# A relational graph layer on one core: S1 T1 by quarters in more calls, and B21 with its sum T4 taken later

## Chip, core and metric

The kernel runs on one core of one Trainium2 chip. The metric is the device time of one execution in microseconds (us); lower is better. The core has a matrix engine (TensorE, PE in the profile; its weight loads are PEld), VectorE (DVE), ScalarE (ACT), GpSimd (POOL) and SyncE (SP). SP, ACT and POOL also issue DMA transfers.

## What is computed

1250 nodes with 1024 features each, 20,000 edges of 8 types. The reference, cut to what matters:

```python
h = jnp.maximum(_layernorm(x, axis=-1), 0.0)
out = h @ root + bias
for r in range(8):
    mask = (edge_type == r).astype(h.dtype)
    sums = jax.ops.segment_sum(h[src] * mask[:, None], dst, num_segments=1250)
    cnt = jax.ops.segment_sum(mask, dst, num_segments=1250)
    out = out + (sums / jnp.maximum(cnt, 1.0)[:, None]) @ weight[r]
u = out
z = jnp.concatenate([u, h], axis=1) @ w_gate + b_gate
result = x + jnp.tanh(u) * z + h * (1.0 - z)
```

Everything is float32. The kernel multiplies first and gathers afterwards: it computes `h @ weight[r]` for all nodes, stores the products in HBM (`y`), and then gathers, for each node, one product row per edge and adds it with its weight.

## The kernel before, in words

**Matrices.** Eleven matrices of 1024 x 1024 are taken one after the other, s = 0 to 10: the eight relation weights (s = 0 to 7), `root` (s = 8), and the two halves of `w_gate` (s = 9, 10). In words they are called matrix one to matrix eleven, so matrix six is s = 5. `R0 = (0, 5, 8)` splits the relations into two groups for the gather: five and three. `EARLY` is 3, `NM` 11, `NP` 5.

**Calls.** The node rows are ten blocks of 128. One call `step(s, i)` with i = 0 to 4 multiplies the block pair (i, i + 5) by matrix s; the first call is i = 0. Each call runs `product`, which is Strassen's scheme in Winograd's form: with the pair's rows as [A11 A12; A21 A22] and the matrix as [B11 B12; B21 B22], all quarters 512 wide, seven products are made in place of eight. The left sums (S1 to S4) were made once and stay in `h_op`; the right sums are made by VectorE for each matrix: T1 = B12 − B11, T2 = B22 − T1, T3 = B22 − B12, T4 = B21 − T2 (`make_t1` to `make_t4`, one instruction each, lines 195 to 207). The products are A11 B11, A12 B21, S1 T1, S2 T2, S3 T3, S4 B22 and A22 T4.

**Where the quarters lie.** Nine buffers of 1 MB hold them. B21 goes into the buffer in which the matrix before had T3; T4 goes into the one in which the matrix before had B22. `load_first`, `load_next`, `load_b22` and `load_b21` bring B11, B12, B22 and B21 of the next matrix during the fourth and fifth call of the present one; the loads of B11, B22 and B21 leave on ScalarE's DMA queue, that of B12 on SP's. In the code, `load_b21` is called at (i, j) = (4, 3) and `make_t4` at (0, 1) of the matrix itself.

**By quarters.** From matrix two on, two calls that follow each other (i = 0 and 1, i = 2 and 3) are paired, and for the two block pairs together some of the seven products are split once more in the same scheme, with 256-wide quarters and seven small products for what would be eight: A12 B21 (class `Second`), S4 B22 (class `Third`, `thirds(s)`, from matrix five on), A11 B11 (class `First`) and S1 T1 (class `Fifth`). `fifths(s, i)` says for which calls the last holds. `Fifth` has a head part, which runs in the first call of the two (`begin`, `second`, `early`, `late`, with `sums` and `next_sums` on VectorE), and leaves the bank `to1` for the other call. In `product` its object is `root`, `Third`'s is `inner`, and `head` is true for i = 0 and 2.

**Banks.** `narrow` is set to `fifths(s, i)`. With it, one of the four rotating PSUM banks is kept (`sum_bank`, `kept`, and `touch`, a short matmul that opens it); without it the bank is given back.

**Order of the work.** All engines run in the order in which the program is written. The schedule is by hand: `product` calls `done()` after each of its products, and `done()` calls `between(j)` with j = 0, 1, 2 and so on. Here that is `beside(j)` in `step`, which places loads, right sums, and the sums of the smaller schemes, and then calls the outer `between`, which places what belongs to the edges. Two more hooks matter. `filled(name)` runs the matmuls of a smaller scheme beside a named product, and makes a further break where that returns true. `between(TICK)` with `TICK` = 9 is an extra break in the head part of a call with `root`.

**First call, from matrix six on.** In order on TensorE: `root.begin()`, the end of `First` (`first.late()`, the bank of p1), `root.second()`, break 0, S2 T2, break 1, `root.early()`, `e.second()` (a quarter product of A12 B21), break 2, S3 T3, the extra break, `root.late()`, break 3, `q.second()` (a quarter product of S4 B22), break 4, A22 T4, break 5. At break 2 and 5 VectorE makes the right sums of `Second` out of B21 (`sums(j)`, line 231); at break 3 it makes the sums of `Third` (`q.sums()`, lines 309 to 312).

**Edges.** While matrices six to eight are multiplied, the rows of the first group are gathered; while nine and ten are multiplied, those of the second. GpSimd issues one indirect DMA for each slot (line 1562, 512 KB, into one of five buffers `got`), and VectorE adds it with a weight to `u` (line 1567). `spread` hands these steps out over the breaks: each break of a call adds 10, 8, 13, 11 or 8 units (by i), and the steps advance to their share of all units; for the first group 123 steps are spread over 1050 units, for the second 88 over 700. On SP run the stores of the products (`put`, line 731), the loads of the bias or of kept partial sums into `u` (line 1580) and the loads of kept left sums (line 243).

Of the kernel before, what the change touches and what calls it, by code (L numbers as in the profile page):

```python
# [21 lines left out]
def tile_rgcn_highway(  # L22
# [44 lines left out]
    NP = ND // 2  # L67
# [3 lines left out]
    R0 = (0, 5, R)  # L71
    K = ((28, 14, 13, 12, 11, 10, 9, 8, 7, 6), (20, 10, 8, 7, 7, 6, 5, 5, 4, 3))
    EARLY = 3
# [10 lines left out]
    TICK = 9  # L84
    LEFTS_AT = 6
    FIFTHS = (1, 4)
# [59 lines left out]
    def lead():  # L146

        return psum.tile([P, 512], F32, name="ps_b", bufs=2)
# [346 lines left out]
    def product(aop, w, to, between=lambda j: None, last=None, pieces=1, whole=True,  # L495
# [13 lines left out]
        def add(b, i, fresh=False, at=slice(0, Q), ks=range(KQ)):  # L509
            for k in ks:  # L510
                nc.tensor.matmul(b[:, at], aop[:, i, k, :], w.of[i][:, k, at],  # L511
                                 start=(fresh and k == 0), stop=(k == KQ - 1),
                                 skip_group_check=True)

        def done():
            between(step[0])
            step[0] += 1

        def filled(name):
            if fill and name in fill and fill[name]():  # L520
                done()
                return True
            return False
# [39 lines left out]
        def p1():  # L563
            if first is None:
                b = lead()
                add(b, A11, True)
            else:
                b = first.late() if head else first.to1
            if root and head:
                root.sums()  # L570
                first.fifth_to()
            nc.scalar.copy(c11, b)  # L572
            if root and head:
                root.second()
            done()
            filled("first")
            return b

        def p5(c=None):
# [14 lines left out]
        if root and head:  # L594
            root.begin()
            c = root.to0
            if inner:
                inner.c0 = c
            b = p1()
        elif first and head and early is None and "first" not in fill:  # L600
            c = inner.hold() if inner else sum_bank(odd) if narrow[0] else bank()
            add(c, S1, True, ks=range(KQ // 2))
            b = p1()
            p5(c)
        elif first and head:
            c = p5()
            b = p1()
        else:
            b = p1()
            if second:  # L610
                second()
                p2()
            c = p5()
# [58 lines left out]
    NM = len(mats)  # L672
    fac = []
# [7 lines left out]
    def thirds(s):  # L681

        return s > EARLY

    def firsts(s):

        return s > 0

    def fifths(s, i=0):

        return s >= FIFTHS[0] and (s <= FIFTHS[1] or i < 2)

    waiting, waiting_third, waiting_first, waiting_fifth = {}, {}, {}, {}
    at_call = [0, 0]
# [9 lines left out]
    def step(s, i, between=lambda j: None, second=None):  # L704

        two = paired(s, i)
        narrow[0] = fifths(s, i)
        if not narrow[0]:
            kept.clear()
# [6 lines left out]
        if two and i % 2 == 0:  # L716
            waiting[i] = Second(fac[s], i), t[0]
            if fifths(s, i):
                waiting_fifth[s, i] = Fifth(fac[s], i, room, p5_room)
# [13 lines left out]
        def beside(j):  # L733
            at_call[:] = i, j
            new = fac[s + 1]
            if i == 0 and s > 0 and j == 1:
                fac[s].make_t4()
            if two and i == 0:
                sums(j)
            if two and i % 2 == 0 and j == 3:  # L740
                if not root:
                    waiting_first[s, i].fifth_to()
                if i == 0 and s == 1:
                    waiting[0][0].left()
                if q:
                    q.sums()
            if q and i % 2 and j == 1:
                q.next_sums()
                q.first_to(to[:, Q:])
            if q and i % 2 and j == 3:  # L750
                q.fifth_to(t[0][:, Q:])
            if coming and (i > 1 or not q) and j == 2:
                first_sums()
            if two and (i, j) == (1, 6) and s == 1:
                Second(fac[s], 2).left()
                Second(fac[s], 2).next_left()
                Second(fac[s], 2).keep_lefts()
            if two and s > 1 and (i, j) == (0, 0):
                waiting[0][0].load_lefts()
            if two and s > 1 and (i, j) == (1, LEFTS_AT):  # L760
                Second(fac[s], 2).load_lefts()
            if (s, i, j) == (0, 0, 3) or (s > 0 and (i, j) == (3, int(thirds(s) or fifths(s)))):
                new.load_first()
            if (s, i, j) == (0, 0, 3) or (s > 0 and (i, j) == (3, 2)):
                new.load_next()
            if i == NP - 1:
                if j == 0:
                    new.load_b22()
                elif j == 1:
                    new.make_t1()  # L770
                elif j == 3:
                    new.load_b21()
                elif j == 4:
                    new.make_t2()
                elif j == 5 and not coming:
                    new.make_t3()
                elif j == 6 and coming:
                    new.make_t3()
            between(j)

        def sums(j):


            e = waiting[0][0]
            for k in {2: (0, 1), 5: (2, 3)}.get(j, ()) if s > EARLY else (j,) if j < 4 else ():
                e.right(k)
            if s == 1 and j == 4:
                e.next_left()
                e.keep_lefts()

        coming = next_first(s, i)
        root = waiting_fifth.get((s, i - i % 2)) if two else None

        def first_sums():
            waiting_first[coming] = First(fac[coming[0]], coming[1], room, p5_room)
            waiting_first[coming].sums()
# [7 lines left out]
        if two:  # L804
# [54 lines left out]
            else:  # L859
                fill = dict(first=lambda: (root and e.fourth(), e.to_second(t[0]),  # L860
                                           e.fourth_to_second(t[0]), 0)[-1],
                            sixth=lambda: (e.second(), True),
                            seventh=lambda: (e.second_to_first(to), put(i - 1, 0, to), 0)[-1])
        product(h_op[i], fac[s], t, between=beside, whole=not two, fill=fill, second=second,
                inner=q, first=waiting_first.get((s, i - i % 2)) if two else None,
                head=i % 2 == 0, lone=i == NP - 1, odd=int(i % 2 or i == NP - 1), root=root,
# [102 lines left out]
    with ExitStack() as early:  # L969
# [20 lines left out]
        class Normed:  # L990
# [13 lines left out]
            def spread(self):  # L1004
                n = self.n
                nc.vector.bn_aggr(self.mv[:n], self.st[:n].rearrange("p a b -> p (a b)"))
                nc.scalar.activation(self.sd[:n], self.mv[:n, 1:2], AF.Sqrt, bias=eps[:n])
# [114 lines left out]
        first = ix1.tile([P, NCH], F32, name="first")  # L1122
# [394 lines left out]
        while going[0]:  # L1517
            s, i = next(steps)
# [11 lines left out]
    with ExitStack() as edges_part:  # L1530
# [89 lines left out]
        def spread(e, total, parts):  # L1620

            said = [0, 0]
            parts *= 10

            def between(j):
                said[0] += (10, 8, 13, 11, 8)[at_call[0]]
                while said[1] < min(total, -(-total * said[0] // parts)):
                    next(e, None)
                    said[1] += 1
                if said[0] == parts:  # L1630
                    for _ in e:
                        pass

            return between
# [36 lines left out]
        def beside(e, total, s, i, last):  # L1671


            between = spread(e, total, 7 * ((last - s) * NP + NP - i))
            while s <= last:
                step(s, i, between)
                s, i = next(steps, (NM, 0))
            return s, i

        s, i = next(steps)  # L1680
        while s <= EARLY:
            step(s, i)
            s, i = next(steps)
# [21 lines left out]
        class Passes:  # L1705
# [45 lines left out]
            def next(self):  # L1751
                nc.vector.tensor_single_scalar(self.done, self.done, float(-MORE), op=OP.add)
# [21 lines left out]
        while s < R0[1]:  # L1774
            step(s, i, on)
            s, i = next(steps)
# [14 lines left out]
        s, i = beside(first_group, sum(K[0]) + LATE + 1, s, i, R0[2] - 1)  # L1791
# [147 lines left out]
        while s < NM - 1:  # L1939
# [8 lines left out]
            s, i = next(steps, (NM, 0))  # L1948
# [86 lines left out]
```

## Time and profile before

| | |
|---|---|
| median of 3 runs | 1325.05 us (1323.67 to 1325.24) |
| the profiled execution | 1326.97 us |
| its span, first to last instruction | 1325.2 us |
| granted TensorE clock, mean | 0.998 |
| VectorE busy | 1031.9 us, 78% |
| GpSimd busy | 637.4 us, 48% |
| HBM traffic | 217 GB/s over the span |
| one matmul row, 128x512 float32 | 3.43 us for eight |
| one gather row on VectorE (line 1567) | 1.28 us |

The profile is of one execution. A timeline lists instructions with their start in us from the span's start and their duration; a matmul's end is modelled and overlaps the next one's start by some 0.16 us. One float32 matmul appears as two rows, so a 512-wide product of a block pair has eight rows and a quarter product four. Line numbers are those of the code above. Instructions of a helper share one line: all large matmuls are on 511, all those of the smaller schemes on 255, so they are told apart by their output and input and their place in time. The granted clock is the share of full clock at which TensorE was allowed to run.

### The profile page before, as it was taken

Reading aid. Unit: us, or ns where it says so; the run is one execution under the profiler, and the core shown is the slowest. Engines: PE = TensorE matmul, PEld = TensorE weight load, DVE = VectorE, ACT = ScalarE, POOL = GpSimd, SP = SyncE. Lnnn points to the kernel's source line nnn. Section 1 sums busy time; section 2 is a strip of 40 time slices with the busy share of each in tenths; the row PEclk is TensorE's granted clock in tenths of the full one; section 3 lists DMA queues with packets and bytes.
Section 4 is the critical chain, followed back from the end, with each engine's and each line's share of the span. In section 5 each row is a group of like instructions: output and inputs, shape, how many; then the busy total and the mean of one; then the engine's idle time right before and its main releaser. Section 6 shows DMA issues by size and latency. Waiting matters only on the chain.

```text
span 1325.2 us, 14354 instructions
## 1 busy us (share of the span) xinstructions
PE 1310.1 (99%) x4280; PEld 746.7 (56%) x4280; DVE 1031.9 (78%) x2171; ACT 277.4 (21%) x509; POOL 637.4 (48%) x981
## 2 busy tenths in 40 slices
PE   9999999999999999999999999999999999999997
PEld 5444565556465546555655665565565566544443
DVE  7768977797783676458987988897788799867974
ACT  3352111122112212211221211122121112222210
POOL 0001766666666675502453545356355556624632
PEclk9999999999999999999999999999999999999999
DMA  8976456762734242244748789888788967979961
GB/s 313 297 234 172 92 114 136 159 81 76 198 84 122 70 122 65 69 159 142 256 133 320 237 286 351 282 273 279 263 279 328 346 215 243 320 273 294 341 168 60
DMA packets 119397, 273.22 MB, mean 206 GB/s; under 512 B 33438, under 2 KB 45106, under 8 KB 119184
## 3 DMA queue, kind: packets, MB, share of 16 engines
q1 hardware_dynamic: 59120, 122.06, 30.7%
q0 software_dynamic: 44064, 118.20, 27.6%
q10 hardware_dynamic: 16128, 31.98, 7.8%
q8 instruction: 34, 0.56, 0.2%
q14 instruction: 51, 0.42, 0.1%
HBM read 210.73 MB, written 76.46 MB: 217 GB/s over the span
## 4 chain that ended last, share of the span: by engine, by line
PE 86%; issue 5%; DVE 3%; DMA 3%; POOL 2%; SPq 1%; ACT 0%; POOLq 0%; DVEq 0%; ACTq 0%
PE ps_b L511 41%; PE ps L255 19%; PE ps L511 11%; PE ps_b L255 4%; PE ps_n L511 3%; PE ps_n L255 3%; PE ps_q L255 2%; PE ps_q L511 2%; DMA xt<-in_x_dram 1%; DMA h_op<-z_dram,node 1%; DMA w<-in_L_gnn_weight_dram 1%; POOL out_dram L903 1%; POOL got L897 1%; DVE row L1959 0%; DVE h_op L1892 0%
## 5 line engine op out<-in xcount | busy, mean ns | idle before, releaser
L511 PE MATMUL ps_b<-w,h_op 128*128 128x512 f32 x1464 | 658.3, 594 | 1.0 <-ACT row L615 0.8
L511 PEld LDWEIGHTS ps_b<-w,h_op 128*128 128x128 f32 x1464 | 275.2, 190 | 301.2 <-issue 292.6
L1562 POOL DMA_INDIRECT got<-y,idx x193 | 249.2, 1291 | 284.5 <-DVE u L1567 182.9
L1567 DVE SCALAR_TENSOR_TENSOR u<-got,w_of,u 128x1024 f32<-128x1024 f32 (+1 forms) x193 | 246.9, 1282 | 37.1 <-DMA got<-y,idx 34.3
L1208 POOL DMA_INDIRECT table<-row_col,at_i x157 | 183.7, 1170 | 118.4 <-issue 85.2
L511 PE MATMUL ps<-w,h_op 128*128 128x512 f32 (+1 forms) x392 | 174.0, 586 | 0.2 <-DVE h_op L492 0.2
L511 PEld LDWEIGHTS ps<-w,h_op 128*128 128x128 f32 x392 | 73.6, 190 | 83.1 <-issue 78.9
L255 PE MATMUL ps<-inner 128*128 128x256 f32 x420 | 106.3, 380 | 0.0
L255 PEld LDWEIGHTS ps<-inner 128*128 128x128 f32 x420 | 79.2, 190 | 21.0 <-issue 9.6
L255 PE MATMUL ps<-w,h_op 128*128 128x256 f32 x340 | 88.3, 382 | 2.3 <-issue 1.3
L255 PEld LDWEIGHTS ps<-w,h_op 128*128 128x128 f32 x340 | 63.6, 190 | 31.0 <-issue 22.9
L537 ACT COPY row<-ps_b 128x512 f32<-128x512 f32 x53 | 31.0, 585 | 223.0 <-PE ps_b L511 213.6
L615 ACT COPY row<-ps_b 128x512 f32<-128x512 f32 x54 | 31.6, 585 | 215.5 <-PE ps_b L511 211.6
L511 PE MATMUL ps_n<-w,h_op 128*128 128x512 f32 x168 | 75.6, 593 | 0.0
L255 PE MATMUL ps<-w,w 128*128 128x256 f32 x288 | 70.6, 380 | 0.0
L255 PEld LDWEIGHTS ps<-w,w 128*128 128x128 f32 x288 | 54.4, 190 | 17.2 <-issue 11.0
L1216 POOL MEMSET apart<- 128x1 f32 x471 | 54.3, 115 | 18.1
L659 ACT COPY row<-ps_b 128x512 f32<-128x512 f32 x40 | 23.4, 584 | 185.1 <-PE ps_b L511 156.4
L543 DVE TENSOR_TENSOR row<-row 128x512 f32<-128x512 f32 x44 | 30.2, 686 | 39.1 <-ACT row L537 39.1
L1325 DVE SCALAR_TENSOR_TENSOR junk<-k_bc,key_col,before 128x128 f32<-128x128 int16 x157 | 55.0, 351 | 4.2
L511 PEld LDWEIGHTS ps_n<-w,h_op 128*128 128x128 f32 x168 | 31.7, 190 | 37.7 <-issue 37.1
L572 ACT COPY row<-ps_b 128x512 f32<-128x512 f32 x54 | 31.7, 587 | 84.0 <-PE ps_b L511 70.0
(257 smaller groups left out, 1568.9 us busy)
## 6 DMA issues: line engine op xcount, KB each, us to landing
y<-row SPq DMA_DIRECT2D x72, 512.0 KB
w<-in_L_gnn_weight_dram ACTq DMA_DIRECT2D x21, 1024.0 KB
w<-in_L_gnn_weight_dram SPq DMA_DIRECT2D x10, 1024.0 KB
w<-lefts_dram SPq DMA_DIRECT2D x16, 512.0 KB
w<-in_L_gnn_w_gate_dram ACTq DMA_DIRECT2D x6, 1024.0 KB
k_bc<-keys_dram SPq DMA_DIRECT2D x39, 128.0 KB
l_bc<-los_dram SPq DMA_DIRECT2D x39, 128.0 KB
h_dram<-h_op SPq DMA_DIRECT2D x9, 512.0 KB
```

The lines of the kernel that those rows point to most:

```text
L255: nc.tensor.matmul(p, a[:, k, :], b[:, k, :], start=(fresh and k == 0), stop=(k == 1), skip_group_check=True)
L511: nc.tensor.matmul(b[:, at], aop[:, i, k, :], w.of[i][:, k, at], start=(fresh and k == 0), stop=(k == KQ - 1), skip_group_check=True)
L537: nc.scalar.copy(d, b)
L543: nc.vector.tensor_add(c22, c if lone else c22, d)
L572: nc.scalar.copy(c11, b)
L615: nc.scalar.copy(c12, b)
L659: nc.scalar.copy(c21, b)
L1208: ins = nc.gpsimd.indirect_dma_start(out=table[:, :], out_offset=bass.IndirectOffsetOnAxis(ap=at_i[:n, c:c + 1], axis=0), in_=row_col[:n, ...
L1216: nc.gpsimd.memset(apart, 0.0)
L1325: nc.vector.scalar_tensor_tensor(junk, o["k_bc"][:, i, :], key_col[:, c:c + 1], before, op0=OP.is_equal, op1=OP.mult, accum_out=rank[:, c: ...
L1562: nc.gpsimd.indirect_dma_start(out=t[:n], out_offset=None, in_=y[g][:, :], in_offset=bass.IndirectOffsetOnAxis(ap=at[:n, d, k:k + 1], axis=0),
L1567: nc.vector.scalar_tensor_tensor(u[:n], t[:n], w, u[:n], op0=OP.mult, op1=OP.add)
```

## The change

`fifths` now holds for all five calls of matrices two to four, for four calls of matrices five to eight, and for two calls of matrices nine and ten. Before it held for all calls of matrices two to five and for two calls of matrices six to ten. So the third and fourth call of matrices six, seven and eight now multiply S1 T1 by quarters, and the fifth call of matrix five, which is alone and not paired, no longer keeps the bank.

A new condition `b21_late(s)` is true for s = 5 to 9, matrices six to ten. For these, `load_b21` is called at break 0 of the matrix's own first call instead of break 3 of the fifth call before, and `make_t4` at break 4 of the first call instead of break 1.

In `product`, a second call of two with `root` and `inner` runs the matmuls beside p1 before the break and not after it. In `spread`, the extra break advances the edges only in the first call.

```diff
@@ -572,8 +572,12 @@
             nc.scalar.copy(c11, b)
             if root and head:
                 root.second()
-            done()
-            filled("first")
+            if root and inner and not head:
+                filled("first")
+                done()
+            else:
+                done()
+                filled("first")
             return b
 
@@ -686,9 +690,13 @@
+    def b21_late(s):
+
+        return EARLY + 1 < s < NM - 1
+
     def fifths(s, i=0):
 
-        return s >= FIFTHS[0] and (s <= FIFTHS[1] or i < 2)
+        return s >= FIFTHS[0] and (s <= EARLY or i < (NP - 1 if s < R0[2] else 2))
 
@@ -733,7 +741,9 @@
         def beside(j):
             at_call[:] = i, j
             new = fac[s + 1]
-            if i == 0 and s > 0 and j == 1:
+            if (i, j) == (0, 0) and b21_late(s):
+                fac[s].load_b21()
+            if i == 0 and s > 0 and j == (4 if b21_late(s) else 1):
                 fac[s].make_t4()
@@ -768,7 +778,7 @@
                     new.load_b22()
                 elif j == 1:
                     new.make_t1()
-                elif j == 3:
+                elif j == 3 and not b21_late(s + 1):
                     new.load_b21()
@@ -1623,7 +1633,8 @@
             def between(j):
-                said[0] += (10, 8, 13, 11, 8)[at_call[0]]
+                if j != TICK or at_call[0] == 0:
+                    said[0] += (10, 8, 13, 11, 8)[at_call[0]]
```

## Prediction

> **What bounds the kernel now.** First I read the page's busy rows, the slices and the chain that ended last.
>
> ```profile
> PE 1310.1 (99%) x4280; PEld 746.7 (56%) x4280; DVE 1031.9 (78%) x2171; ACT 277.4 (21%) x509; POOL 637.4 (48%) x981
> ...
> PE   9999999999999999999999999999999999999997
> ...
> PE 86%; issue 5%; DVE 3%; DMA 3%; POOL 2%; SPq 1%; ACT 0%; POOLq 0%; DVEq 0%; ACTq 0%
> ```
>
> TensorE is busy in every slice. From 8.67 us to the last matmul its rows show only seven idle spans over 0.15 us, the longest 1.30 us. So nothing that makes another engine faster can pay, matmuls taken out pay in full, and every wait put in front of a matmul is paid in full. I therefore followed what stands in front of each matmul at the two places that the change moves: the use of B21 and the use of T4 in the first call of a matrix. The engines' timelines in the first call of matrix seven (s = 6), TensorE first:
>
> ```profile
> 737.90 1.89 PE L255 MATMUL ps<-inner 128*128 128x256 f32 x8
> 739.62 1.03 PE L255 MATMUL ps<-w,h_op 128*128 128x256 f32 x4
> 740.49 3.60 PE L511 MATMUL ps_b<-w,h_op 128*128 128x512 f32 x8
> ...
> 745.88 1.13 PE L255 MATMUL ps<-inner,h_op 128*128 128x256 f32 x4
> 746.85 1.03 PE L255 MATMUL ps_n<-w,h_op 128*128 128x256 f32 x4
> 747.71 3.60 PE L511 MATMUL ps_b<-w,h_op 128*128 128x512 f32 x8
> ```
>
> The columns are start, duration, engine, line, operation, output and inputs. At 739.62 `e.second()` reads a quarter of B21. From 740.49 S3 T3 runs, then `root.late()`, whose last product starts at 745.88; at 746.85 `q.second`; at 747.71 A22 T4, the product that reads T4. VectorE over the same time:
>
> ```profile
> 737.76 2.28 DVE L207 TENSOR_TENSOR w<-w,w 128x2048 f32<-128x2048 f32 x1
> ...
> 747.53 0.43 DVE L445 TENSOR_TENSOR ps<-ps,inner 128x256 f32<-128x256 f32 x1
> 747.87 0.68 DVE L543 TENSOR_TENSOR row<-row 128x512 f32<-128x512 f32 x1
> 748.46 0.42 DVE L309 TENSOR_TENSOR inner<-h_op 128x256 f32<-128x256 f32 x1
> 748.80 0.71 DVE L310 TENSOR_TENSOR inner<-w 128x512 f32<-128x512 f32 x1
> 749.43 0.41 DVE L311 TENSOR_TENSOR inner<-inner,h_op 128x256 f32<-128x256 f32 x1
> 749.77 0.68 DVE L312 TENSOR_TENSOR inner<-w,inner 128x512 f32<-128x512 f32 x1
> 750.37 3.91 DVE L1567 SCALAR_TENSOR_TENSOR u<-got,w_of,u 128x1024 f32<-128x1024 f32 x3
> ```
>
> L207 is `make_t4`: finished at 740.04, it lies 7.7 us ahead of its reader. L445 and L543 are the tail of the fourth break's product, L309 to L312 its `q.sums()`, L1567 gathered rows being added.
>
> **T4 at the fifth break.** In the first call the breaks come after p1 (j = 0), S2 T2 (1), `e.second` (2), S3 T3 (3) and `q.second` (4); A22 T4 is the very next product after break 4. `make_t4` is one instruction over all of T4, and VectorE works in written order, so before it stand L445, L543, the four sums and what break 3 advances of the gathers. L445 adds to the bank that `root.late()` fills: in matrix five, where VectorE had been idle before it, it starts at 561.92, 0.11 us after the product's end at 561.81. In matrix seven that is 747.01 + 0.11 = 747.12. From L445's start to L312's end the rows take 750.45 − 747.53 = 2.92 us. Break 3 brings one L1567: 123 gather steps over 1050 units, and units 400 and 410 of this call's 390, 400, 410 round up to 47 and 49 after 46, so one step at break 3, two at break 4; at starts 1.2 us apart that adds 1.20. T4 adds 2.28 less 0.08 of overlap, 2.20. Its end is 747.12 + 2.92 + 1.20 + 2.20 = 753.44; A22 T4 could have started at 747.71, so TensorE waits 5.7, with 0.06 for the release **5.8 us**. Taking T4 away from 737.76 doesn't shorten this: VectorE would then only wait for `root.late()` at 747.12. Matrices six, eight and nine show the same rows (L445 at 632.25, 862.67, 978.00, A22 T4 at 632.46, 862.85, 978.26). In matrix ten VectorE is late already (L445 at 1095.73, A22 T4 at 1093.40): its chain would end T4 at 5.8 after the product if the 2.28 us given back make up that lag, near 8.7 if the lag is the gathers' own; I take 7.0. Sum 4 × 5.8 + 7.0 = **30.2 us**; bounds 5 × 4.6 = 23 (no gather step ahead of T4) and 5 × 8.7 = 43.5 (gathers late everywhere). Behind T4 on VectorE wait the second pair of B21's right sums (L231) and break 4's gather steps; their readers come 6 us and more later and TensorE waits as well, so nothing further.
>
> **B21 at the first break.** The load leaves ScalarE's queue with the copy of C11 (L572, 732.82), as today's loads leave beside the copies of their breaks, and `e.second` reads it at 739.62: 6.8 us later. It is 1 MB. Stretches by time (length, then busy time of PE, PEld, DVE, ACT, POOL, granted clock, DMA share, GB/s): that window, the window after a B22 load with nothing else in flight, and one in which a load met gathers and stores:
>
> ```profile
> core 0: us, PE busy (x) PEld busy (x) DVE busy (x) ACT busy (x) POOL busy (x), PEclk, DMA share, GB/s
> ...
> 732.83:739.62 6.79, 6.79 (x24) 4.47 (x24) 6.75 (x9) 1.53 (x3) 2.53 (x2) 1.00 0.79 237
> ...
> 591.20:596.20 5.00, 5.00 (x13) 2.15 (x12) 1.58 (x1) 0.57 (x1) 0.00 (x0) 1.00 0.63 210
> ...
> 821.30:832.40 11.10, 11.10 (x27) 4.88 (x27) 7.84 (x8) 1.17 (x2) 4.41 (x5) 1.00 1.03 409
> ```
>
> Alone, the load lands 4.6 us after its issue (its traffic is over by 596.0): no wait. But the new window already carries 1.61 MB at a DMA share of 0.79 (two y stores, the lefts and a bias block, all on SP). With 1.05 MB more it is 2.66 MB, at 300 (237 ÷ 0.79) to 409 GB/s 8.9 to 6.5 us, and the load's traffic starts 1.1 us after issue: landing 7.6 to 10 us after it, less where it is served before the rest. The windows of matrices six, eight, nine and ten have shares 0.79, 0.99, 0.88 and 0.55. I take a wait of 1.9 us in four matrices and 0.4 in ten, **8 us**; bounds 0 and, for a landing after 11.1 us as around 821, 5 × 4.3 = 21.5. Behind this wait everything in the call shifts alike, so T4's wait comes on top of it. The place that B21 leaves (fourth break of the fifth call) gives nothing: no matmul waited there. On ScalarE the issue takes 0.4 us ahead of a copy that comes 5 us later.
>
> **The clock after the waits.** At the end the trace shows what an idle TensorE does: its last matmul ends at 1317.33 and the granted clock is halved 2.66 us later; at the start it runs at half from 1.37 to 5.86 us.
>
> ```profile
> 1317.40:1319.98 2.58, 0.00 (x0) 0.00 (x0) 0.81 (x2) 0.00 (x0) 2.05 (x3) 1.00 0.64 242
> 1319.99:1325.20 5.21, 0.00 (x0) 0.00 (x0) 0.00 (x0) 0.00 (x0) 0.00 (x0) 0.50 0.06 19
> ```
>
> A wait of 5.8 us is longer than 2.66. If the clock then needs as long as at the start, 4.5 us at half, 2.24 us of work is lost. The 1.3 us waits of matrix five changed nothing, so B21's alone would not. With four of the five halved: **9 us**; bounds 0 and, 3 us each, 15. The Trainium skill ("TensorE: Matmul & The Clock Gate", Part 1) puts the fall differently: only a whole idle window of about 3.4 us, free-running, halves the clock, so a 5.8 us wait would hold one 7 times in 10; estimated by that page the term is 5 × 0.7 × 2.24 = 7.8 us, by the row alone 11.2.
>
> **S1 T1 by quarters in the third and fourth call of matrices six to eight.** Two blocks take 16 matmul rows of 512 columns, 2 × 3.43 us (734.47 to 737.90); by quarters seven groups of four at 0.863: 6.04. Gain 0.83 per matrix, **−2.5 us**. VectorE gets eight sums and two adds more, 2 × 2.19 + 0.85 = 5.2 us. In those two calls it is busy 34.6 of 42.4 us; 39.8 of 41.6 would still be under the 44.5 of 45.2 that calls one and two bear with TensorE waiting for nothing. ScalarE gets 1.3 us and has 8.6 of 42.4. Without that room each microsecond would be paid. In matrix five, whose third and fourth calls already run so, one wait of 1.25 us stands at 560.68. I take 0.5 each, **1.5 us**, bounds 0 and 9.
>
> **Nothing or nearly so.** The fifth call of matrix five was not multiplied by quarters and only changes banks; the bank kept from it is touched anew in matrix six, one 0.2 us matmul. The `filled`/`done` swap puts a break's gather steps behind the inner products: in second calls these use VectorE not at all, in fourth calls it moves adds past each other. The third call's extra break doesn't advance the gathers, so their pace stays.
>
> **Sum.** 30.2 + 8 + 9 − 2.5 + 1.5 + 0.2 = 46.4 us on the profiled 1325.2 us span (1326.97 around it; the median of the runs, 1325.05, lies as near): 1371 us, range 1345 to 1392.
>
> **Rivals.** (1) Only T4 waits: B21 lands in time and the clock holds. For it: 4.6 us alone, and waits near the length that halves. 1325 + 30.2 − 0.8 = 1354 us; chance 0.15. (2) The loads collide as around 821: 21.5 in place of 8 gives 1384 us, and gathers held up behind it more; the share of 0.99 in matrix eight speaks for it, 0.55 in ten against; 0.13. (3) The other side: T4 is not late, because VectorE is through it before A22 T4 is due, and B21 lands inside 6.8 us. Then only −2.5 + 1.5 + 0.2, or −2.3 with no friction, is left: 1323 to 1324 us. It decides once L445 to T4's end fits into the 0.86 us of `q.second`; the rows say 6.3. The same time results if the late order were not taken at all, which the conditions on s exclude for six to ten. Together 0.04.
>
> **Chances.** Forecast (1358 to 1381) 0.68, the rivals 0.15, 0.13, 0.04. 0.2% (2.7 us) is about what runs of this kernel can tell apart. Faster 0.02, same 0.02, slower 0.96.
>
> **What would show it.** In matrices six to ten the first 128x512 matmul after the `ps_n` quarter of the first call should show TensorE idle some 5.8 us, released by DVE L207, L207 directly behind one L1567; the `ps<-w,h_op` quarter before S3 T3 some 0 to 4 us, released by the weight DMA; PEclk below 1.00 after the former; six to eight 0.83 us shorter in calls three and four. I am wrong if A22 T4 starts without a gap, or if either wait is made up later.

## The result, and the profile after

| | before | after |
|---|---|---|
| median of the runs side by side | 1324.67 us (4 runs) | 1394.83 us (4 runs, 1393.86 to 1397.45) |
| ratio | | 1.0537, 95% interval 1.0525 to 1.055 |
| profiled execution, its span | 1326.97, 1325.2 us | 1394.35, 1392.6 us |
| mean granted TensorE clock | 0.998 | 0.979 |

The change makes the kernel 5.4% slower, 70.2 us. The forecast was 1371 us with a range of 1345 to 1392: the direction and the places of the two waits are as predicted, the time lies 2.8 us above the range.

The page of the changed kernel, the same rows as before and the clock beside them (each digit is a tenth, for 40 equal slices):

```profile
PE 1329.7 (95%) x4317; PEld 762.8 (55%) x4317; DVE 1048.2 (75%) x2201; ACT 281.0 (20%) x518; POOL 651.9 (47%) x981
...
PE   9999999999999999988998899699979998999997
...
PEclk9999999999999999998999999899989999999999
...
PE 82%; DMA 7%; issue 4%; DVE 4%; POOL 1%; SPq 1%; ACT 0%; POOLq 0%; DVEq 0%; ACTq 0%
```

From the eighteenth slice on, where matrices six to ten are multiplied, TensorE has slices that are not full, and the granted clock dips beside them. DMA has gone from 3% to 7% of the chain, VectorE from 3% to 4%. The list of what TensorE waited for says how much (us in total, how often, the longest):

```profile
PE ps_b L511 <- DVE w L207: 28.0, 5, 5.7
PE ps L255 <- DMA w<-in_L_gnn_weight_dram: 17.2, 3, 7.6
PE ps L255 <- DMA w<-in_L_gnn_root_dram: 4.4, 1, 4.4
PE ps L255 <- DMA w<-in_L_gnn_w_gate_dram: 1.5, 1, 1.5
```

The first line is T4 (L207 is `make_t4`), once in each of matrices six to ten. The other three are B21 in the same five: matrices six to eight are relation weights, nine is `root`, ten the first half of `w_gate`. In the first call of matrix seven, TensorE first, then VectorE (start, duration, and in brackets the idle time before it and what ended it):

```profile
750.34 1.89 PE L255 MATMUL ps<-inner 128*128 128x256 f32 x8
755.79 1.13 PE L255 MATMUL ps<-w,h_op 128*128 128x256 f32 x4 [3.56 <-DMA w<-in_L_gnn_weight_dram]
756.76 3.60 PE L511 MATMUL ps_b<-w,h_op 128*128 128x512 f32 x8
...
762.15 1.13 PE L255 MATMUL ps<-inner,h_op 128*128 128x256 f32 x4
763.12 1.03 PE L255 MATMUL ps_n<-w,h_op 128*128 128x256 f32 x4
769.74 6.08 PE L511 MATMUL ps_b<-w,h_op 128*128 128x512 f32 x8 [5.59 <-DVE w L207]
```

```profile
763.39 0.43 DVE L445 TENSOR_TENSOR ps<-ps,inner 128x256 f32<-128x256 f32 x1 [2.16 <-PE ps L255]
...
765.60 0.68 DVE L312 TENSOR_TENSOR inner<-w,inner 128x512 f32<-128x512 f32 x1
766.21 1.28 DVE L1577 SCALAR_TENSOR_TENSOR u<-got,w_of,u 128x1024 f32<-128x1024 f32 x1
767.40 2.28 DVE L207 TENSOR_TENSOR w<-w,w 128x2048 f32<-128x2048 f32 x1
```

These are the same matmuls as before, with two holes in them: 3.56 us ahead of `e.second()`, 5.59 ahead of A22 T4. VectorE stands idle until `root.late()` has ended (763.28), then goes through L445, L543, the four sums, one gathered row (L1577, formerly L1567) and T4, in that order. And A22 T4, eight rows that took 3.60 us, takes 6.08: the clock is down.

**Where 70 us went.** All idle time ahead of the two uses is 28.0 + 23.1 us; a row's modelled end overlaps the next start by 0.16 us, so each wait cost 0.16 more: 28.8 + 23.9. The granted clock is halved eight times, for 6.83 us each; half of TensorE's busy time within the halved stretches is lost, 2.0 to 3.0 us each, 19.9 together. The quarters give 2.5 back. 28.8 + 23.9 + 19.9 − 2.5 = 70.1, against 70.2 between the medians. (The spans differ by only 67.4, because the profiled execution of before has two waits of 1.3 us in matrix five that no later profile has.)

### The profile page after: what moved, and what is told of

It reads as the page before. It is cut to its first block, busy times and chain, and to the rows that moved or that the text cites. A ratio compares the mean times of both kernels' runs of the same rounds, so it can differ in the third digit from the quotient of the medians.

```text
span 1392.6 us, 14466 instructions
## 1 busy us (share of the span) xinstructions
PE 1329.7 (95%) x4317; PEld 762.8 (55%) x4317; DVE 1048.2 (75%) x2201; ACT 281.0 (20%) x518; POOL 651.9 (47%) x981
## 4 chain that ended last, share of the span: by engine, by line
PE 82%; DMA 7%; issue 4%; DVE 4%; POOL 1%; SPq 1%; ACT 0%; POOLq 0%; DVEq 0%; ACTq 0%
PE ps_b L511 40%; PE ps L255 19%; PE ps L511 9%; DMA w<-in_L_gnn_weight_dram 3%; PE ps_b L255 3%; PE ps_n L511 3%; PE ps_n L255 3%; PE ps_q L255 2%; PE ps_q L511 2%; DMA xt<-in_x_dram 1%; DMA got<-hr_dram,node 1%; DMA w<-in_L_gnn_root_dram 1%; DVE w L207 1%; DMA w<-in_L_gnn_w_gate_dram 1%; POOL out_dram L913 1%
## 5 line engine op out<-in xcount | busy, mean ns | idle before, releaser
L511 PE MATMUL ps_b<-w,h_op 128*128 128x512 f32 x1464 | 675.5, 607 | 29.0 <-DVE w L207 28.0
L511 PEld LDWEIGHTS ps_b<-w,h_op 128*128 128x128 f32 x1464 | 282.3, 195 | 339.5 <-issue 301.0
L1572 POOL DMA_INDIRECT got<-y,idx x193 | 257.8, 1336 | 331.4 <-DVE u L1577 239.8
L1577 DVE SCALAR_TENSOR_TENSOR u<-got,w_of,u 128x1024 f32<-128x1024 f32 (+1 forms) x193 | 246.7, 1281 | 35.4 <-DMA got<-y,idx 32.9
L511 PE MATMUL ps<-w,h_op 128*128 128x512 f32 (+1 forms) x368 | 163.2, 585 | 0.1
L255 PE MATMUL ps<-w,h_op 128*128 128x256 f32 x352 | 94.6, 392 | 24.1 <-DMA w<-in_L_gnn_weight_dram 17.2
L255 PE MATMUL ps<-inner 128*128 128x256 f32 x456 | 114.9, 380 | 0.0
L255 PEld LDWEIGHTS ps<-inner 128*128 128x128 f32 x456 | 86.3, 190 | 22.6 <-issue 8.6
L255 PE MATMUL ps<-w,w 128*128 128x256 f32 x288 | 70.1, 380 | 0.0
L511 PE MATMUL ps_n<-w,h_op 128*128 128x512 f32 x144 | 64.8, 593 | 0.0
L543 DVE TENSOR_TENSOR row<-row 128x512 f32<-128x512 f32 x44 | 30.2, 687 | 27.3 <-ACT row L537 27.3
```

Of the source, the lines that this page charges most:

```text
L255: nc.tensor.matmul(p, a[:, k, :], b[:, k, :], start=(fresh and k == 0), stop=(k == 1), skip_group_check=True)
L543: nc.vector.tensor_add(c22, c if lone else c22, d)
L1572: nc.gpsimd.indirect_dma_start(out=t[:n], out_offset=None, in_=y[g][:, :], in_offset=bass.IndirectOffsetOnAxis(ap=at[:n, d, k:k + 1], axis=0),
L1577: nc.vector.scalar_tensor_tensor(u[:n], t[:n], w, u[:n], op0=OP.mult, op1=OP.add)
```

## The experiments

**S1 T1 alone.** Everything of the change but the late B21 and T4:

```diff
     def b21_late(s):
-        return EARLY + 1 < s < NM - 1
+        return False
```

> B21 and T4 are taken as in the kernel before; the rest of the change stays (S1 T1 by quarters, the swap, the pace). Theory (the whole loss is in the late B21 and T4): no wait is put ahead of a matmul, 3 x 0.83 = 2.5 us of matmuls go, and the two waits of 1.3 us in matrix five, which are missing in the changed kernel too, may go as well: span 1320 to 1323 us against 1325.2. Rival (VectorE, with 5.2 us more in calls three and four, makes TensorE wait): 1326 us or more, with idle spans released by VectorE in the third and fourth call of matrices six to eight.

1321.02 us (11 runs) against 1323.81, ratio 0.9981, interval 0.9972 to 0.999. Calls three and four of matrix six take 41.59 us in place of 42.43, the 0.83 that the rows said. After the start of the kernel the one new wait is 0.28 us at 945.70, for L310 of VectorE. So the quarters bring what their rows said, and the whole loss is in the late half. It has the lowest median measured here, below both kernels; the version with B21 ahead, further down, lies within 0.9 us of it. Below, "quarters alone" means this one.

**The two late parts, one at a time.** First T4 alone at the fifth break, with B21 loaded in the call before, as ever:

```diff
-            if (i, j) == (0, 0) and b21_late(s):
-                fac[s].load_b21()
...
-                elif j == 3 and not b21_late(s + 1):
+                elif j == 3:
                     new.load_b21()
```

> B21 is loaded as in the kernel before, T4 is made at the fifth break. Theory (each wait costs its own length and, where it halves the clock, half of what TensorE does until the clock is back): five waits of 5.76 us, 28.8, and five halvings that cost 2.4 to 3.0 each in the changed kernel, 13.4, less about 5 for S1 T1 and matrix five: 1325.2 + 28.8 + 13.4 - 5 = 1362 us. Rival (a halving needs the B21 wait ten us earlier as well, or T4 is late only because the call is late): 1349 us or less.

1363.01 us, ratio 1.0296 (1.0277 to 1.0315). The list of waits has one new line:

```profile
PE ps_b L511 <- DVE w L207: 28.9, 5, 6.5
```

The clock is halved five times, for 11.0 us. Then B21 alone at the first break, with T4 at the third, the first break after the product that reads B21:

```diff
-            if i == 0 and s > 0 and j == (4 if b21_late(s) else 1):
+            if i == 0 and s > 0 and j == (2 if b21_late(s) else 1):
                 fac[s].make_t4()
```

> B21 is loaded at the first break as in the changed kernel, T4 is made at the third break, right behind the product that waits for B21. Theory: VectorE is through T4 some 4 us before A22 T4 is due, so T4's waits and their halvings go; B21's waits stay with their 23.9 us in all (1.5 to 7.6 each), and three halvings with 6.5: 1325.2 - 5 + 23.9 + 6.5 = 1351 us. Rival (T4 is late wherever it stands in this call, since VectorE is full): an idle span released by line 207 before A22 T4 remains, and the time is over 1360 us.

1353.12 us, ratio 1.0221 (1.0203 to 1.024). No wait for T4; the five for B21 are 6.16, 5.70, 7.37, 2.88 and 1.59 us, and four of them halve the clock, for 6.9 us. Over the quarters alone the two parts cost 42.0 and 32.1 us, together 74.1, and the changed kernel 73.8: they add up, within the 1 us or so by which the kernel before differs from one group of runs to the next (medians of 1323.03 to 1324.67). A cover for the one would not have hidden the other. In matrix ten T4's wait is 6.49 us in T4 alone and 5.65 in the changed kernel: with B21 in time, VectorE starts L445 there 0.99 us after `root.late()` and not 0.10.

**Late parts without the quarters.** `fifths` as before, the rest of the change kept:

```diff
-        return s >= FIFTHS[0] and (s <= EARLY or i < (NP - 1 if s < R0[2] else 2))
+        return s >= FIFTHS[0] and (s <= FIFTHS[1] or i < 2)
```

> S1 T1 by quarters only where the kernel before has it; B21 and T4 late as in the changed kernel. Theory (the loss is all in the late B21 and T4, the quarters take their 2.5 us off): the changed kernel's 1394.8 plus 2.5, 1397 us, give or take 4 for the loads' landings. Rival (VectorE's extra sums in calls three and four make the late loads dearer): 1390 us or less.

1396.31 us (1392.95 and 1399.67), ratio 1.0549 (1.0518 to 1.058). It lies 1.5 us above the changed kernel, with overlapping intervals. That agrees with quarters that keep their 2.5 us also beside the waits, but two runs can't show it.

**Is it the clock?** Six 512-wide products of the identity with a broadcast zero column are added into the bank of A22 T4 before it, in the first call of matrices six to ten. They add nothing to the sums, need nothing from VectorE and fill the wait with work:

```diff
+            if root and head and zeros[0]:
+                for _ in range(6):
+                    nc.tensor.matmul(b, ident, zero.to_broadcast([P, Q]), start=False, stop=False,
+                                     skip_group_check=True)
```

On the changed kernel:

> The changed kernel, with six matmuls of a zero operand, 512 columns wide, ahead of A22 T4 in the first call of matrices six to ten; they add nothing to the sum and fit into the wait for T4. Theory (the wait halves the clock): the five granted clocks of 0.5 at A22 T4 go, and with them 13.4 us, while the time at which A22 T4 starts after q.second stays 5.8 us: 1392.6 - 13.4 = 1379 us, mean clock above 0.985. Rival (what is slow after the wait is not the clock but late operands or VectorE): 1391 us or more.

1386.99 us (1383.01 and 1390.97; 1379 was expected), ratio 1.0477 (1.0449 to 1.0506). All halvings after T4 are gone and the loss to the clock falls from 19.9 to 9.9 us. But the profiled run, the slower one, had longer waits for B21 (25.3 us in place of 23.1) and a new one of 3.32 us at 860.97, behind a VectorE that had waited 7.8 us for a gather; that one halved the clock as well. So on top of B21's uncertain waits the test was blurred, and it was made again on T4 alone:

> t4_alone, with six matmuls of a zero operand ahead of A22 T4 in the first call of matrices six to ten; they add nothing to the sum. Theory (the clock): A22 T4 starts as late as in t4_alone, the five halvings go and with them 11.0 us: span 1360.8 - 11.0 = 1350 us, time 1352 against 1363. Rival (the 11 us are something else, such as VectorE being behind after the wait): 1360 us or more.

1352.15 us (1350.82 to 1355.94), ratio 1.0212 (1.0195 to 1.0229): 10.9 us faster than T4 alone, by matmuls that compute nothing. In matrix six:

```profile
627.93 1.03 PE L255 MATMUL ps_n<-w,h_op 128*128 128x256 f32 x4
628.80 5.33 PE L661 MATMUL ps_b<-zero,ident 128*128 128x512 f32 x12
634.55 3.70 PE L511 MATMUL ps_b<-w,h_op 128*128 128x512 f32 x8 [0.42 <-DVE w L207]
```

L661 is the filling. A22 T4 still starts only when T4 is there (0.42 us are left to wait), 6.62 us after `q.second` as in T4 alone, but its eight rows take 3.70 us, near the 3.60 of the full clock. None of the five waits for T4 halves the clock any more. The profiled execution, the longest of the four, has one other halving, for 1.7 us, after a wait of 3.30 us for VectorE at 965.71. The clock's share of T4's cost is shown, not only argued: 11 of 42 us.

**Why is B21 so late?** In the changed kernel's profile the five stretches from the issue of the load to its use (start and end, length, then busy time with counts for PE, PEld, DVE, ACT, POOL, granted clock, DMA share, GB/s):

```profile
614.08:627.14 13.06, 6.96 (x24) 4.30 (x24) 9.21 (x40) 1.54 (x3) 5.53 (x5) 0.89 0.98 343
745.27:755.79 10.52, 6.96 (x24) 4.29 (x23) 8.56 (x14) 1.53 (x3) 4.12 (x3) 1.00 0.99 331
871.63:886.16 14.53, 6.97 (x25) 4.30 (x24) 9.25 (x14) 1.54 (x3) 7.79 (x4) 0.92 1.01 364
1004.47:1015.81 11.34, 6.96 (x25) 4.30 (x24) 5.07 (x14) 1.53 (x3) 6.10 (x6) 0.90 0.99 347
1135.19:1143.65 8.46, 6.96 (x25) 4.29 (x24) 8.39 (x13) 1.53 (x3) 4.46 (x3) 1.00 0.76 247
```

TensorE has 6.96 us of work in each; what is longer is wait. The DMA share is 0.98 to 1.01 in the first four: all 16 engines are full, and not with B21 alone. Beside its 1.05 MB, SP's queue moved 1.54, 1.56, 1.81, 1.38 and 1.02 MB and the gathers 1.89, 0.87, 2.42, 1.49 and 0.02 MB. Five edits of "B21 alone" take this apart.

*Issued where nobody needs it soon.* The load leaves at the seventh break of the fifth call of the matrix before, some 6 us earlier, and no more at break 0:

```diff
-            if (i, j) == (0, 0) and b21_late(s):
-                fac[s].load_b21()
...
+                if j == 6 and b21_late(s + 1):
+                    new.load_b21()
```

> b21_alone, with the load of B21 called at the last break of the fifth call, where ScalarE reaches it some 6 us sooner and SP has not yet issued the stores, the lefts and the bias block. T4 stays at the third break. Theory (the load is slow because it queues with SP's 1.5 to 2 MB): it lands 5 to 8 us after its issue, 12.8 us before its use, no wait is left, and the time is that of s1t1_alone, 1320 to 1322 us. Rival (loads at this point take 8.5 to 14.5 us whatever stands before them): waits of 1 to 2 us remain in two or three matrices, 1323 to 1327 us.

1321.88 us (10 runs), ratio 0.9987 (0.9977 to 0.9997). No wait for B21, no halving; it lands 4.4 to 7.3 us after its issue, and its first data come after 1.0 to 1.4 us. In matrix six it leaves at 607.95 and is read at 620.77, 12.8 us later in place of 7: issuing it 6 us earlier takes away 31 of the 32 us of B21 alone. The earlier issue gives the load more time and also puts it ahead of SP's transfers; this run doesn't part the two. A wait of 1.44 us for L310 of VectorE at 946.33 is left.

*On SP's queue, behind the stores that are there* (here and below `load_b21` and `load_lefts` take the queue as an argument):

```diff
-                fac[s].load_b21()
+                fac[s].load_b21(nc.sync)
```

> b21_alone, with B21's load at the same place in the program but on SP's queue, where it is issued behind the two y stores and ahead of the lefts and the bias block. Theory (the load is last because on ScalarE's queue it shares the DMA engines with all that SP has sent already and then with the gathers): some 1.0 MB of stores and its own 1.05 MB at 0.36 MB per us take 5.6 us from about 2 us before the first break, 4 to 5 us after it, against the 6.8 that e.second leaves: no wait or under 1 us in each matrix, no halving, 1320 to 1326 us. Rival (any load that starts here lands 8 us or more later, by its own descriptors): waits of 1 to 6 us remain, 1335 us or more.

1333.68 us, ratio 1.0069 (1.0054 to 1.0084). The waits fall to 1.81, 1.43, 3.81, 2.17 and 0.69 us, one of them halves the clock. Neither theory's number: on SP's queue, ahead of the left sums and the bias, 13.8 of the 23.7 us of waits go, and the rest stays. The issue itself moves little: it is 0.2 to 1.0 us earlier, measured from the time at which TensorE could read, in matrices six, seven and ten, and 0.4 and 1.2 us later in eight and nine.

*The left sums after it.* `load_lefts` was written at the fourth break in place of the first, still on SP:

```diff
-            if two and s > 1 and (i, j) == (0, 0):
+            if two and s > 1 and (i, j) == (0, 3 if b21_late(s) else 0):
                 waiting[0][0].load_lefts()
```

> b21_alone, with the load of the kept lefts (0.5 MB on SP) moved from the first to the fourth break of the call in matrices six to ten. Theory (the load shares the DMA engines with what SP sends in that window): 0.5 MB less at 0.3 MB per us is up to 1.7 us less wait in each matrix, 5 to 8 us in all: span 1343 to 1346 us against 1350.8. Rival (its end is set by the gathers that start 8 us after its issue and by their share of the DMA engines): 1349 to 1352 us.

1357.37 us (1354.73 and 1360.0). The edit missed its aim. SP's queue in matrix seven, of B21 alone and then of this kernel (start, duration of the issues, the transfer):

```profile
734.54 0.78 SPq L739 DMA_DIRECT2D y<-row  x2
735.41 0.70 SPq L243 DMA_DIRECT2D w<-lefts_dram  x1
736.16 2.08 SPq L1590 DMA_DIRECT2D u<-in_L_gnn_bias_dram  x1
```

```profile
734.35 0.79 SPq L739 DMA_DIRECT2D y<-row  x2
735.19 0.74 SPq L1590 DMA_DIRECT2D u<-in_L_gnn_bias_dram  x1
736.02 1.90 SPq L243 DMA_DIRECT2D w<-lefts_dram  x1
```

The left sums (L243) only changed places with the bias (L1590) and left 0.6 us later, long before the fourth break. SP has nothing but transfers to issue, and nothing that it issues here waits for a break; so an order in the program is on SP an order among its own transfers and no place in time. The waits (6.00, 6.03, 6.98, 4.56, 0.84) say that in them it is B21 alone once more; the two runs lie 5 us apart.

*The left sums on ScalarE's queue at the fourth break*, where the copies of the products hold the issue back:

```diff
-            if two and s > 1 and (i, j) == (0, 0):
-                waiting[0][0].load_lefts()
+            if two and s > 1 and (i, j) == (0, 3 if b21_late(s) else 0):
+                waiting[0][0].load_lefts(nc.scalar if b21_late(s) else nc.sync)
```

> b21_alone, with the kept lefts loaded on ScalarE's queue at the fourth break, where ScalarE's copies hold it back until e.second has run; on SP it was issued at once whatever its break. Theory (all bytes under way before the landing count): 0.52 MB less at 0.36 MB per us is 1.4 us less wait in each of the five matrices, 5 to 7 us, and a halving may go too: span 1342 to 1346 us against 1350.8. Rival (the load's end is set by the gathers alone): 1349 to 1353 us.

1342.6 us, ratio 1.0146 (1.0127 to 1.0164). The waits, first of B21 alone, then of this kernel:

```profile
PE ps L255 <- DMA w<-in_L_gnn_weight_dram: 19.2, 3, 7.4
PE ps L255 <- DMA w<-in_L_gnn_root_dram: 2.9, 1, 2.9
PE ps L255 <- DMA w<-in_L_gnn_w_gate_dram: 1.6, 1, 1.6
```

```profile
PE ps L255 <- DMA w<-in_L_gnn_weight_dram: 11.4, 3, 7.1
PE ps L255 <- DMA w<-in_L_gnn_root_dram: 2.3, 1, 2.3
PE ps L255 <- DMA w<-in_L_gnn_w_gate_dram: 1.3, 1, 1.3
```

With 0.53 MB taken out of the window, matrices six and seven wait 2.1 and 2.2 us in place of 6.2 and 5.7; matrix eight stays at 7.05, where 2.48 MB of gathers come with the load. The time is the theory's, but not for its reason: it had 1.4 us less in each of the five, and the runs show 4.0, 3.5, 0.3, 0.6 and 0.3. In six and seven the window that is now shorter also holds 1.15 and 0.89 MB less of gathers; so the load gains more there than the bytes taken out. And the left sums now make TensorE wait themselves once, 0.94 us at 995.30.

*The gathers held back.* The edges are not advanced at breaks 0 and 1 of the first call, and twice at 4 and 5:

```diff
-                    said[0] += (10, 8, 13, 11, 8)[at_call[0]]
+                    said[0] += ({0: 0, 1: 0, 4: 20, 5: 20}.get(j, 10) if at_call[0] == 0
+                                else (10, 8, 13, 11, 8)[at_call[0]])
```

> B21 at the first break and T4 at the third, as in the run of B21 alone (1353 us; waits for B21 6.2, 5.7, 7.4, 2.9, 1.6 us in matrices six to ten), but the edges are not advanced at breaks 0 and 1 of the first call, and by twice as much at breaks 4 and 5. In matrices seven, eight and ten this takes away the added rows of the first two breaks, and with them the gathers that GpSimd issues as each added row frees a buffer; matrices six and nine, whose gathers begin a new part of the work and wait for no added row, stay as controls. Theory, the gathers delay the load by their bytes: 1.48 MB less in matrix seven at 0.33 MB a microsecond, and about 1.4 of 2.42 MB less in eight, so the waits fall from 5.7 to 1 to 2 us and from 7.4 to 3 to 4.5 us, matrix seven's clock holds, and the time is 1340 to 1345 us. Rival, the load is late for what lies ahead of it on the engines, stores and loads of the left sums, and the gathers that start 4 to 7 us after it no longer matter: the waits of seven and eight stay within 1 us and the time at 1350 us or more. If rows of VectorE that come later make TensorE wait, that shows as waits released by VectorE.

In matrix seven no gather is left in the window and the wait falls from 5.70 to 3.20 us; in eight 1.05 MB are left and it falls from 7.37 to 4.73; six stays (5.93). So the gathers cost 2.5 and 2.6 us there, not the 4 or so that their bytes over the bandwidth would give, and not nothing. The window of matrix seven without them:

```profile
736.61:746.77 10.16, 6.96 (x24) 4.29 (x23) 4.81 (x11) 1.54 (x3) 0.00 (x0) 1.00 0.75 256
```

Even so the load needs 10.16 us, at a DMA share of only 0.75: 2.6 MB are not served as a block at full rate, and the load's first data come 2.6 us after its issue, where B21 ahead had 1.0 to 1.4. As a whole the kernel gained nothing, 1356.04 us (1.0256, 1.0225 to 1.0286): nine and ten waited 1.0 and 1.4 us longer, every one of the five waits now halved the clock (8.5 us for 6.9), and the rows that came later made TensorE wait for L316 (2.8 us in four waits). Of the time, the rival was right; of the waits, neither: the theory had them shorter by 3.7 to 4.7 and 2.9 to 4.4 us, the rival by less than 1.

**Could more quarters pay?** On the quarters alone, also the third and fourth call of matrices nine and ten:

```diff
-        return s >= FIFTHS[0] and (s <= EARLY or i < (NP - 1 if s < R0[2] else 2))
+        return s >= FIFTHS[0] and (s <= EARLY or i < (NP - 1 if s < NM - 1 else 2))
```

> s1t1_alone, with S1 T1 by quarters in the third and fourth call of matrices nine and ten too. Theory (two more times 0.83 us of matmuls go and VectorE bears the 5.2 us): 1.7 us less than s1t1_alone's 1321.0, 1319 to 1320 us. Rival (in matrix ten the gathers already hold VectorE up, and the longer list of sums makes TensorE wait): 1321 us or more.

1325.37 us (11 runs), ratio 1.0013 (1.0003 to 1.0023), 4.4 us above the quarters alone. TensorE now waits for VectorE:

```profile
PE ps L255 <- DVE inner L310: 3.4, 2, 1.8
PE ps L255 <- DVE row L283: 2.3, 2, 1.5
PE ps L255 <- DVE inner L316: 1.9, 1, 1.9
```

The execution profiled is the longest of the eleven. The wait at 946.38 (1.68 us, L310) is in the fifth call of matrix eight, which the edit leaves as it was, and stands, 0.28 and 1.44 us long, in the profiles of the quarters alone and of B21 ahead as well. The other four lie in matrices nine and ten. Before three of them (0.83 us at 1033.35, 1.75 at 1063.71, 1.46 at 1155.02) VectorE had itself been idle for a gather that had not landed: 3.19, 1.73 and 3.29 us. Only the one at 1089.42 (1.87 us), in the first call of matrix ten, comes behind a VectorE that was busy throughout. In time the rival was right; of its two reasons the gathers show, the longer list of sums does not by itself. On the whole VectorE has room: in the kernel before it is busy for 31.67 and 35.58 of the 42.43 us of calls three and four there, 33.5 to 34.6 in matrices six to eight. It works in written order, and where it stands behind a late gather, the sums behind it are late too. Whether the added quarters make the gathers late is not shown.

## Why the prediction was right, and where it was wrong

**T4 at the fifth break: right.** Forecast 5.8 us in four matrices and 7.0 in ten, 30.2; measured 5.59 four times and 5.65, with the overlap 28.8. L445 starts 0.11 us after `root.late()` as worked out, and the chain behind it is the one that was added up, link by link: row, sums, one gather step, T4. In matrix ten, where VectorE had been late before by 2.9 us, the wait came out as the lower of the two cases named, but not for the reason given: the 2.28 us given back made up only 2.0 of them, as T4 alone shows with its 6.49 us, and the wait of 1.5 us for B21 covered the rest. That was luck.

**S1 T1: right.** −2.5 forecast, −2.8 between the medians of the quarters alone and before. Of the 1.5 us of friction 0.28 came, in the fifth call of matrix eight.

**B21 at the first break: here the prediction failed.** The step that failed is the time from the load's issue to its landing. "I take a wait of 1.9 us in four matrices and 0.4 in ten, 8 us"; measured 23.9, beyond the upper bound of 21.5 too. Behind it stood a landing 7.6 to 10 us after the issue; in matrices six to ten the load's last data came 12.5, 10.0, 14.0, 10.8 and 8.1 us after it. The window was sized as "2.66 MB, at 300 … to 409 GB/s 8.9 to 6.5 us", from what stood in the 6.8 us of the old window. Two things were wrong in that. A wait makes the window longer, and what had come after it now falls into it: the gathers, which begin some 7 us after the issue in matrices six and seven and about with it in eight and nine, and were worth 2.5 us where they were held back. And all bytes of the window were taken to be served at one rate from 1.1 us after the issue on; with no gather at all, 2.6 MB took 10.2 us at a share of 0.75, with the load's first data at 2.6 us and 1.56 MB of SP's in the same window. Taking the left sums out, or B21 on SP's queue ahead of them, was worth 8.7 and 13.8 us in all. How much of the rest is the start and how much the order of service is open.

**The clock after the waits: the second step that failed, in part from the first.** "With four of the five halved: 9 us", upper bound 15; measured 19.9. The kind of loss was right and its mean size near (2.24 forecast, 2.5 measured), the latter with some luck: the clock stayed halved for 6.83 us each time, not 4.5, but up to 2.8 us of that fell into the wait itself. The count was wrong. All five waits for T4 halved the clock, and so did the three for B21 of 4.38 us and more, which were not thought of as halving since they were thought to be 1.9 long. Nor are the 2.66 us at the end of the trace a length that halves the clock: waits of 1.87 and 2.28 us did it in two of the runs, and one of 3.56 did not (see the last section).

**Rivals.** The second one, loads that collide, was nearest: 1384 us, with 21.5 us for B21. It still counted the clock at 9. The first (only T4 waits, 1354) is what T4 alone would be with a clock that held, and the chip gave that too: 1352. The third, no wait at all, fell with the first A22 T4.

**Range.** With the two terms at their upper bounds, 21.5 and 15, and all else as forecast the sum is 1391, about where the range ended; the measured 23.9 and 19.9 lie beyond both. The terms are not independent: a longer wait for B21 also halves the clock more often.

## What to carry to other kernels

Where TensorE is 99% busy, a wait is paid in full and, if it is long enough, a second time through the clock: 1.5 to 3.1 us were lost behind it. In these profiles no wait under 1.87 us halved the clock and every one of 3.65 us or more did. When a load is moved close to its use, count what the window will hold once it has grown, gathers that start later included, and try the issue some breaks earlier before anything else: here that took 31 of 32 us away. An engine that only issues transfers, as SP here, can run ahead of the place where its lines are written; to tie a transfer to a moment, give it to an engine that has work at that moment.

## What the runs showed of the chip

**The clock gate keeps a fixed grid.** In eleven profiles here the clock is halved 44 times outside the start and the end. Within one execution all halvings begin at multiples of 3.413 us from one another. Cut on that grid, TensorE's busy share tells which stretch halves the clock. Around the wait of 3.56 us, the wait of 5.59 and the wait of 4.38 in the changed kernel:

```profile
750.66:754.07 3.41, 1.57 (x8) 1.04 (x6) 2.68 (x6) 0.84 (x2) 2.69 (x3) 1.00 1.00 369
754.07:757.49 3.42, 1.70 (x6) 1.25 (x7) 1.09 (x3) 0.00 (x0) 0.00 (x0) 1.00 0.95 364
764.32:767.73 3.41, 0.00 (x0) 0.00 (x0) 3.41 (x7) 0.00 (x0) 0.39 (x1) 1.00 0.83 278
767.73:771.15 3.42, 1.41 (x2) 0.84 (x3) 3.38 (x3) 0.00 (x0) 2.81 (x2) 0.50 0.20 80
771.15:774.56 3.41, 3.41 (x5) 1.35 (x4) 3.41 (x4) 0.00 (x0) 2.91 (x2) 0.50 0.73 185
1010.07:1013.49 3.42, 1.36 (x7) 0.86 (x5) 1.95 (x5) 0.63 (x2) 2.81 (x3) 1.00 1.00 375
```

A stretch with TensorE busy for 1.57 us (46%) leaves the clock alone, one with 1.36 us (40%) or none halves it from its end on (767.73, 1013.49). Over all profiles, of the stretches that begin at full clock, every one up to 42% halved it and none from 46% on did; of two between, one at 44% did not and one at 45% did. The half clock then lasts through the first stretch that is busy for 86% or more; stretches of up to 80%, as from 767.73 to 771.15, did not end it. So it lasted one, two or three stretches, and a loss is half of what TensorE did in them. This is why the two holes of 3.56 and 4.38 us differ, and why 2.88 us could be enough in B21 alone: the split by the grid decides. Counted from the first instruction the grid lies elsewhere in each execution (its lines at 3.15 us and multiples of 3.413 later in the changed kernel, at 0.93 in T4 alone). The Trainium skill ("TensorE: Matmul & The Clock Gate", Part 1) has the free-running window of about 3.4 us, and the runs agree. What it calls an idle window may here be filled up to some 45%: all fifteen waits for T4 in the three kernels with T4 late and nothing to fill them (5.58 to 6.49 us) halved the clock, where, estimated by a window idle throughout, as the prediction reads that page, some three in ten would have passed.

**One set of DMA engines.** B21 on ScalarE's queue was slowed by transfers that SP and GpSimd had issued, by 2.5 us for the gathers in matrix seven, and by 3.5 us there for 0.53 MB of left sums and the gathers that the longer window then took in. That agrees with the Trainium skill ("DMA: Bandwidth & Descriptors", "Issuing engines are not separate DMA queues"), by which transfers from all engines interleave on the same 16 DMA engines. A queue of its own did not keep B21 clear of them.

**Left open.** How much of B21's lateness comes from its late start and how much from the order in which transfers are served was not found out. The two waits of 1.3 us in matrix five, put down to "issue" in the profiled execution of before, stand in none of the later profiles; what they are was not found out either.
